# Row sums of the first head group moved from TensorE matmuls to accumulating transfers and VectorE, in a two-layer graph attention kernel

## The chip, the cores and the metric

The kernel runs on one core of a Trainium2 chip. The metric is the device time of one execution in microseconds. The version before takes 3048.53 us, the median of 3 runs (3048.48 to 3050.49).

A core has TensorE (PE, matmuls into PSUM), VectorE (DVE), ScalarE (ACT), GpSimd (POOL) and SyncE (SP). Each takes its own instructions in order and waits on semaphores for the others. Transfers are issued here from SP and from GpSimd.

## The reference

Thirty-two graphs of 512 nodes with 256 features pass two layers. `adj` is a 0/1 matrix for each graph. All arithmetic is float32.

```python
# layer 0, per graph
allowed = (adj > 0) | (adj.T > 0) | eye
q, k, v = split(x @ Wqkv.T + bqkv)                # 8 heads of 32
attn    = softmax(where(allowed, q k^T / sqrt(32), -inf))
x1      = layernorm(x + (attn v) @ Wo.T + bo) * g1 + b1
ff      = relu(x1 @ W1.T + b1) @ W2.T + b2        # hidden width 1024
x2      = layernorm(x1 + ff) * g2 + b2
x       = layernorm(x + x2)
# layer 1, per graph: attention alone, masked where adj == 0
x       = layernorm(x + attention(x, adj))
```

## The kernel before

Matrices lie with 128 rows on the 128 partitions. The eight heads form two head groups `hg` of four, so that four 32-wide heads fill the partitions. Scores are computed transposed: `scores(layer, k)` makes, for head group `k // 4` and key block `k % 4`, a 128 (keys) x 4 heads x 512 (queries) tile `s` in PSUM (L399). `exp` (ScalarE, L408) writes it to an SBUF tile `p` of 1 MB, of which there are eight buffers; `s` has one buffer, so the next scores wait for the exp. `masked` (VectorE, L412) multiplies by the 0/1 mask, and `product` (L419) accumulates values times `p` over the four key blocks into `acc`. `context` copies `acc` to `cT`.

No maximum is subtracted; the quotient is applied to `cT` at the end. The row sums run over keys, that is over the partitions and the four blocks. For each layer and head group:

- `pair` (L432), an accumulating transfer issued by GpSimd, adds one `p` tile to another; `fold` (VectorE, L435) does the same. For group 0 blocks 0 to 3 end in the tile k=2 by two pairs and a fold; for group 1 blocks 4 to 7 end in k=3's buffer by a pair and two folds.
- `sums` (L443) multiplies the folded tile by a 128x32 block of ones: four matmuls, one per head, whose result `psR` holds each head's sums repeated on 32 partitions.
- `blocks` (VectorE, L460) transposes 32x32 blocks of it into `sT`, `invert` (L463) takes the reciprocal of one column, `widen` (L471) spreads it back over 32 partitions, `divide` (L475) multiplies `cT`. `sT` has one buffer, which `blocks` and `widen` share.
- `guard` (GpSimd, L467) adds the sums and the reciprocals to a running `total`; at the end a total that isn't below a limit switches to a general version of the kernel.

In the last layer of the last graph there is no folding: `sums` runs over all four tiles.

`project` multiplies by Wo, `add`, `stats`, `aggregate`, `root` (GpSimd), `center` and `affine` are the residual and the layer norm, `hidden`, `relu` and `mlp` the feed-forward part. Dense products go through `dense` (L186) and are either one 128-wide matmul (`wide=True`) or four 32-wide ones. Their PSUM tiles share three banks with `psR`.

The order of all work is written out by hand as a list of such calls. `opening` (L551) starts the pipeline, `period` (L1366) is called 26 times with five neighbouring graphs a to e in different states, and `closing` (L1657) ends it. Nothing reorders them: each engine takes its own calls in the order of that list. A transfer is issued from the queue of the engine that its method names.

```python
folded = [2 + hg] if not self.final(layer) else range(hg * NQ, (hg + 1) * NQ)
for k in folded:
    for j in range(HPC):
        nc.tensor.matmul(ps[j * HD : (j + 1) * HD, :], ones, self.p(layer, k)[:, j, :], ...)
```

Of the kernel before, what the change touches and what calls it, by code (L numbers as in the profile page):

```python
# [27 lines left out]
def kernel(ctx: ExitStack, tc: tile.TileContext, t: dict, out: bass.AP):  # L28
# [12 lines left out]
    nc = tc.nc  # L41
# [109 lines left out]
    def plain(pools: ExitStack):  # L151
# [7 lines left out]
        def value_bias(layer):  # L159
            ps = ps_d.tile([P, D], F32, tag="d", name=f"psB_{layer}")  # L160
            bv = proj[layer][3]
            for k in range(ND):
                nc.tensor.matmul(
                    ps, bv[:, k : k + 1].to_broadcast([P, P]), wo[layer][:, k, :], start=(k == 0), stop=(k == ND - 1)
                )
            nc.vector.tensor_tensor(bov[layer], ps, bo[layer], ALU.add)

        def hidden_bias():

            ps = ps_d.tile([P, NF], F32, tag="d", name="psB_2")  # L170
            for f in range(NF):
                for c in range(ND):
                    nc.tensor.matmul(  # L173
                        ps[:, f : f + 1],
                        w1[:, c, f * P : (f + 1) * P],
                        b2_c[:, c : c + 1],
                        start=(c == 0),
                        stop=(c == ND - 1),
                    )
            nc.vector.tensor_tensor(b1, b1, ps, ALU.subtract)  # L180
            nc.vector.tensor_tensor(be1, be1, b2, ALU.add)

        def dense(out, lhsT, rhs, start, stop, wide):

            for at in (slice(0, P),) if wide else [slice(j * HD, (j + 1) * HD) for j in range(HPC)]:
                nc.tensor.matmul(out[at], lhsT[:, at], rhs, start=start, stop=stop)  # L186

# [4 lines left out]
        class Graph:  # L192
# [121 lines left out]
            def once(self, i):  # L314

                if i < 2:
                    value_bias(i)
                else:
                    hidden_bias()
# [131 lines left out]

            def sT(self, layer, hg):
                return self.at("sT", (layer, hg), [N // HD, HD], bufs=1)

# [3 lines left out]
            def blocks(self, layer, hg):  # L458

                nc.vector.transpose(self.sT(layer, hg).rearrange("p a b -> p (a b)"), self.bank("R", (layer, hg), [N]))  # L460

            def invert(self, layer, hg):
                nc.vector.reciprocal(self.r(layer, hg), self.sT(layer, hg)[:, :, 0])  # L463

            def guard(self, layer, hg, i):
                src = self.r(layer, hg) if i else self.sT(layer, hg)[:, :, 0]
                nc.gpsimd.tensor_tensor(total, total, src, ALU.add)  # L467
# [83 lines left out]
        def opening(a, b, c, d, e):  # L551

            a.load()
            a.constants(0, 4)
            a.transpose(0, 0)
            a.transpose_out(0, 0)
            a.transpose(0, 1)
            a.transpose_out(0, 1)
            a.query_key(0, 0, 0, None, wide=True)
            a.query_key(0, 1, 0, None, wide=True)  # L560
            b.flip(0)
            b.sort(0, 1, 0)
            b.sort(0, 0, 0)
            a.query_key_out(0, 0, 0, None)
            a.query_key_out(0, 1, 0, None)
            a.scores(0, 1)
            a.query_key(0, 0, 1, None)
            a.constants(22, 23)
            a.exp(0, 1)
            a.query_key_out(0, 0, 1, None)  # L570
            a.scores(0, 3)
            a.exp(0, 3)
            a.query_key(0, 1, 1, None)
            a.query_key_out(0, 1, 1, None)
            b.flip(1)
            a.scores(0, 0)
            a.exp(0, 0)
            b.sort(0, 0, 1)
            a.cast()
            a.entries()  # L580
            a.entry(1)
            a.entry(0)
            b.cast()
            a.entry(2)
            b.join(0, 0)
            a.value(0, 1)
            a.scores(0, 2)
            a.exp(0, 2)
            a.entry(3)
            a.masks(0)  # L590
            a.value_out(0, 1)
            a.masks(1)
            b.sort(0, 1, 1)
            b.sort(1, 0, 0)
            a.value(0, 0)
            b.sort(1, 1, 0)
            a.value_out(0, 0)
            a.scores(0, 4)
            a.exp(0, 4)
            a.constants(10, 12)  # L600
            b.sort(1, 0, 1)
            a.masks(2)
            b.join(1, 0)
            a.masked(0, 0)
            a.scores(0, 7)
            a.product(0, 0)
            a.masked(0, 1)
            a.masked(0, 2)
            b.sort(1, 1, 1)
            b.join(1, 1)  # L610
            a.product(0, 1)
            a.pair(0, 0)
            a.product(0, 2)
            a.masked(0, 3)
            a.pair(0, 2)
            a.exp(0, 7)
            a.scores(0, 5)
            a.product(0, 3)
            b.join(0, 1)
            a.exp(0, 5)  # L620
            b.query_key(0, 0, 1, None)
            a.context(0, 0)
            a.masked(0, 7)
            b.query_key(0, 0, 0, None)
            a.constants(4, 6)
            a.scores(0, 6)
            a.masked(0, 4)
            b.query_key_out(0, 0, 0, None)
            a.product(0, 4)
            a.masked(0, 5)  # L630
            b.value(0, 1)
            b.query_key(0, 1, 0, None)
            b.query_key_out(0, 0, 1, None)
            a.exp(0, 6)
            a.masked(0, 6)
            b.query_key_out(0, 1, 0, None)
            a.product(0, 5)
            b.query_key(0, 1, 1, None)
            a.fold(0, 2, 2, 0)
            a.sums(0, 0)  # L640
            a.fold(0, 3, 6, 7)
            a.pair(0, 4)
            b.scores(0, 2)
            b.query_key_out(0, 1, 1, None)
            b.value(0, 0)
            b.exp(0, 2)
            a.constants(6, 8)
            a.product(0, 6)
            b.value_out(0, 1)
            a.blocks(0, 0)  # L650
            a.guard(0, 0, 0)
            a.product(0, 7)
            a.constants(8, 10)
            a.invert(0, 0)
            a.widen(0, 0)
            a.fold(0, 3, 3, 4)
            a.sums(0, 1)
            a.divide(0, 0)
            a.blocks(0, 1)
            a.guard(0, 1, 0)  # L660
            b.scores(0, 1)
            a.context(0, 1)
            c.flip(1)
            a.once(0)
            b.entry(1)
            a.invert(0, 1)
            a.widen(0, 1)
            a.divide(0, 1)
            a.project(0, 0, wide=True)
            b.exp(0, 1)  # L670
            b.value_out(0, 0)
            a.bias(1)
            a.project(0, 1, wide=True)
            a.add(1, 0)
            a.stats(1, 0)
            a.once(2)
            a.add(1, 1)
            a.aggregate(1, 0)
            b.entry(2)
            a.stats(1, 1)  # L680
            a.aggregate(1, 1)
            a.add(1, 3)
            a.root(1, 0, 2)
            a.center(1, 1)
            a.add(1, 2)
            a.affine(1, 1)
            a.center(1, 0)
            b.scores(0, 0)
            a.affine(1, 0)
            a.transpose(1, 0)  # L690
            a.transpose_out(1, 0)
            a.hidden(0, 4, wide=True)
            a.stats(1, 2)
            b.exp(0, 0)
            a.relu(0, 5)
            b.entry(0)
            a.hidden(0, 6, wide=True)
            a.relu(0, 4)
            a.hidden(0, 2, wide=True)
            a.stats(1, 3)  # L700
            a.relu(0, 2)
            a.relu(0, 6)
            a.relu(0, 7)
            a.aggregate(1, 3)
            a.aggregate(1, 2)
            a.root(1, 2, 4)
            c.sort(1, 1, 0)
            a.center(1, 2)
            b.entries()
            a.relu(0, 3)  # L710
            a.affine(1, 2)
            a.hidden(0, 0, wide=True)
            a.center(1, 3)
            a.affine(1, 3)
            a.transpose(1, 1)
            b.entry(3)
            b.masks(0)
            a.relu(0, 0)
            b.masks(1)
            a.relu(0, 1)  # L720
            a.masks(3)
            b.masks(2)
            b.masked(0, 0)
            b.scores(0, 5)
            b.exp(0, 5)
            a.mlp(0)
            b.masked(0, 1)
            a.constants(12, 14)
            a.bias(0)
            b.masked(0, 2)  # L730
            b.scores(0, 3)
            b.masked(0, 5)
            a.mlp(1)
            a.add(2, 1)
            c.cast()
            a.stats(2, 1)
            a.aggregate(2, 1)
            a.transpose_out(1, 1)
            a.hidden(1, 2)
            a.relu(1, 3)  # L740
            a.relu(1, 2)
            a.add(2, 0)
            a.stats(2, 0)
            b.exp(0, 3)
            c.flip(0)
            a.hidden(1, 0)
            a.relu(1, 1)
            a.hidden(1, 4)
            d.cast()
            a.hidden(1, 6)  # L750
            a.relu(1, 6)
            c.sort(0, 1, 0)
            a.center(2, 1)
            a.aggregate(2, 0)
            c.entry(0)
            a.root(2, 0, 2)
            b.product(0, 0)
            b.product(0, 1)
            a.affine(2, 1)
            b.product(0, 2)  # L760
            a.stats(3, 1)
            a.center(2, 0)
# [2027 lines left out]
```

## Time and profile before

| | |
|---|---|
| median of 3 runs | 3048.53 us |
| the profiled execution | 3046.83 us |
| its span, first to last instruction | 3044.7 us |
| mean granted TensorE clock | 0.997 |
| busy PE, DVE, ACT, POOL | 3006.8, 2667.0, 1736.5, 947.7 us |
| one repeat of `period` (start of one output store to the next) | 93.2 us |
| psR matmuls (L443) | 1072 records, 139.7 us busy |
| accumulating transfers of `p` | 189 of 1 MB, 7.7 us to landing |

A float32 matmul leaves two records, so the 1072 records are 536 matmuls or 134 packs of four, whose four matmuls, one for each column group, run side by side. The busy time of an engine is the time in which at least one of its instructions runs; neighbours overlap a little, so the start of the next instruction comes before the end of the last.

### The profile page before, as it was taken

How to read it: one execution, taken by the hardware profiler on the slowest of the kernel's cores; microseconds unless marked ns; L12 is line 12 of the kernel's file. 1: busy time of each engine (PE TensorE's matmuls, PEld its weight loads, DVE VectorE, ACT ScalarE, POOL GpSimd, SP SyncE). 2: the span in 40 equal slices, each digit the busy share in tenths (PEclk: the TensorE clock that was granted, in tenths of full speed). 3: DMA queues.
4: the chain of work that ended last, by engine and by line, in shares of the span. 5: the costliest groups of instructions: out<-in, count | busy, mean ns of one | idle time of the engine just before them, and what ended most of it. 6: DMA issues, size and time to landing. Idle time of an engine off the chain costs nothing.

```text
span 3044.7 us, 85990 instructions
## 1 busy us (share of the span) xinstructions
PE 3006.8 (99%) x38410; PEld 1359.9 (45%) x38410; DVE 2667.0 (88%) x3524; ACT 1736.5 (57%) x2111; POOL 947.7 (31%) x1126
## 2 busy tenths in 40 slices
PE   7999999999999999999999999999999999999997
PEld 3444444444444444444444444444444444444443
DVE  4788888989888998889898898988898988988986
ACT  4555655556555555655555555556555665555554
POOL 0122333333333333333333333333333333332221
PEclk9999999999999999999999999999999999999999
DMA  7554445555455654555554455544564544554440
GB/s 164 115 111 107 104 100 109 120 112 107 94 109 110 126 110 93 102 109 124 106 108 96 108 116 120 110 97 99 109 129 103 105 100 105 119 121 100 81 91 23
DMA packets 257017, 325.32 MB, mean 107 GB/s; under 512 B 147329, under 2 KB 231425, under 8 KB 231937
## 3 DMA queue, kind: packets, MB, share of 16 engines
q0 software_dynamic: 28240, 214.97, 35.7%
q1 hardware_dynamic: 228400, 104.79, 14.8%
q8 instruction: 303, 4.96, 0.7%
q14 instruction: 74, 0.60, 0.1%
HBM read 72.23 MB, written 33.55 MB: 35 GB/s over the span
## 4 chain that ended last, share of the span: by engine, by line
PE 97%; ACT 1%; DMA 1%; DVE 0%; issue 0%; POOL 0%; SPq 0%; DVEq 0%; ACTq 0%
PE s L399 18%; PE acc L419 15%; PE psH L186 15%; PE psF L186 15%; PE psQK_None L186 11%; PE psO L186 7%; PE psV L186 7%; PE psR L443 4%; PE psQK L186 4%; PE psT L360 2%; ACT p L408 1%; DMA p<-p 0%; DMA w_L_gnn_Wqkv<-in_L_gnn_Wqkv_dram 0%; PE psB L173 0%; DVE p L435 0%
## 5 line engine op out<-in xcount | busy, mean ns | idle before, releaser
L408 ACT ACTIVATE p<-s 128x2048 f32<-128x2048 f32 x512 | 962.9, 1881 | 558.7 <-PE s L399 484.6
L412 DVE TENSOR_TENSOR p<-p,m 128x2048 f32<-128x2048 f32 x512 | 1160.5, 2274 | 40.3 <-ACT p L408 37.5
L399 PE MATMUL s<-qT,kT 32*64 32x512 f32 x8192 | 571.2, 613 | 4.9 <-ACT p L408 4.0
L419 PE MATMUL acc<-p,v 128*32 128x512 f32 x4096 | 513.7, 597 | 1.3 <-DVE p L412 1.3
L504 POOL TENSOR_SCALAR rs<-mv 128x2 f32<-128x2 f32 (+1 forms) x320 | 276.4, 864 | 700.0 <-DVE mv L499 663.3
L186 PE MATMUL psH<-xT,w_L_gnn_W 128*32 128x256 f32 (+1 forms) x8024 | 480.4, 380 | 0.7 <-ACT xT L365 0.7
L186 PE MATMUL psF<-w_L_gnn_W,hT 128*32 128x256 f32 x6704 | 466.2, 380 | 0.0
L435 DVE TENSOR_TENSOR p<-p,p 128x2048 f32<-128x2048 f32 x189 | 427.6, 2275 | 2.6 <-DMA p<-p 2.2
L467 POOL TENSOR_TENSOR total<-total,sT 128x16 f32<-128x16 f32 x128 | 191.8, 1498 | 703.6 <-DVE mv L499 399.7
L540 ACT ACTIVATE hT<-psH,c_L_gnn_b 128x256 f32<-128x256 f32 x512 | 217.5, 475 | 304.6 <-PE psH L186 293.5
L186 PEld LDWEIGHTS psH<-xT,w_L_gnn_W 128*32 128x32 f32 (+1 forms) x8024 | 262.3, 111 | 268.6 <-issue 46.2
L186 PEld LDWEIGHTS psF<-w_L_gnn_W,hT 128*32 128x32 f32 x6704 | 287.3, 116 | 197.5 <-issue 36.4
L432 POOL DMA_DIRECT2D p<-p x189 | 171.0, 905 | 653.2 <-PE acc L419 458.9
L505 POOL TENSOR_TENSOR rs<-rs,neg_half 128x2 f32<-128x2 f32 (+1 forms) x320 | 257.8, 806 | 26.7
L399 PEld LDWEIGHTS s<-qT,kT 32*64 32x64 f32 x8192 | 119.3, 130 | 310.7 <-issue 143.7
L186 PE MATMUL psQK_None<-xT,w_L_gnn_Wqkv 128*32 128x512 f32 (+1 forms) x1988 | 241.0, 595 | 4.7 <-DMA w_L_gnn_Wqkv<-in_L_gnn_Wqkv_dram 4.7
L186 PE MATMUL psO<-w_L_gnn_Wo,cT 128*32 128x256 f32 (+1 forms) x2056 | 238.5, 380 | 2.9 <-DVE cT L475 2.9
L419 PEld LDWEIGHTS acc<-p,v 128*32 128x32 f32 x4096 | 114.3, 109 | 257.8 <-issue 189.2
L186 PEld LDWEIGHTS psO<-w_L_gnn_Wo,cT 128*32 128x32 f32 (+1 forms) x2056 | 168.8, 136 | 65.7 <-issue 12.9
L496 DVE BATCH_NORM_STATS2 st<-y 128x6 f32<-128x256 f32 x384 | 158.4, 420 | 6.2
L365 ACT COPY xT<-psT 128x512 f32<-128x512 f32 x130 | 75.9, 583 | 140.1 <-PE psT L360 140.1
L493 DVE TENSOR_TENSOR y<-psO,x 128x256 f32<-128x256 f32 x256 | 102.9, 413 | 51.9 <-PE psO L186 51.4
(71 smaller groups left out, 2777.6 us busy)
## 6 DMA issues: line engine op xcount, KB each, us to landing
p<-p POOLq DMA_DIRECT2D x189, 1024.0 KB, 7.7
x<-in_x_dram SPq DMA_DIRECT2D x32, 512.0 KB, 4.2
code<-in_adj_dram POOLq DMA_DIRECT2D x32, 512.0 KB, 9.9
m<-code SPq DMA_DIRECT2D x32, 512.0 KB, 4.6
out_dram<-x SPq DMA_DIRECT2D x32, 512.0 KB, 3.8
kT<-v SPq DMA_DIRECT2D x248, 64.0 KB, 3.0
m<-code SPq DMA_TRANSPOSE x128, 4.0
w_L_gnn_W<-in_L_gnn_W_dram SPq DMA_DIRECT2D x2, 1024.0 KB, 9.4
```

Of the source, the lines that this page charges most:

```text
L186: nc.tensor.matmul(out[at], lhsT[:, at], rhs, start=start, stop=stop)
L399: nc.tensor.matmul(s[half * P // 2 : (half + 1) * P // 2, j, :], self.kT(layer)[at, hg, key : key + P // 2], self.qT(layer)[at, hg, :], st ...
L408: nc.scalar.activation(self.p(layer, k), self.at("s", (layer, k), [HPC, N]), AF.Exp, scale=SCALE)
L412: nc.vector.tensor_tensor(p, p, m[:, k % NQ, None, :].to_broadcast([P, HPC, N]), ALU.mult)
L419: nc.tensor.matmul(acc[j * HD : (j + 1) * HD, :], self.v(layer)[:, kc, h * HD : (h + 1) * HD], self.p(layer, k)[:, j, :], start=(kc == 0), ...
L432: nc.gpsimd.dma_start(out=self.p(layer, k), in_=self.p(layer, k + 1), accum_op=ALU.add)
L435: nc.vector.tensor_tensor(self.p(layer, dst), self.p(layer, a), self.p(layer, b), ALU.add)
L467: nc.gpsimd.tensor_tensor(total, total, src, ALU.add)
L496: nc.vector.bn_stats(self.at("st", (n, i), [6]), self.y(n, i))
L504: nc.gpsimd.tensor_scalar(rs, self.mv(n)[:, a:b, 1:2], EPS, None, ALU.add)
L505: nc.gpsimd.tensor_tensor(rs, rs, neg_half[:, a:b, None], ALU.pow)
L540: nc.scalar.activation(self.hT(h)[:, f, :], ps[:, f % 2, :], AF.Relu, bias=b1[:, f : f + 1])
```

## The change

Group 0 of both layers no longer uses TensorE for its sums, except in the last layer of the last graph. The folded tile is halved twice by accumulating transfers (`halve`: partitions 64 to 127 are added to 0 to 63, then 32 to 63 to 0 to 31). Four transfers (`spread`) lay head j's 32 partitions at partitions 32j of a tile `part`. `blocks` transposes `part`, and a new VectorE reduction (`reduce`) sums 32 values for each query into a small tile `total`, which `invert` and `guard` then read. Group 1 keeps its matmul. In the last layer of the last graph group 0 keeps it too, and `reduce` is a copy there.

The constants that were computed in one call (`value_bias`, `hidden_bias`) are split into a TensorE part (`once`) and a VectorE part (`once_out`). The lists `opening`, `period` and `closing` are written anew throughout: order of key blocks, of projections, of transfers, and which dense products are wide.

```diff
+        SPREAD = {(0, 0), (1, 0)}
...
+            def spread_out(self, layer, hg):
+                return (layer, hg) in SPREAD and not self.final(layer)
+
+            def halve(self, layer, hg, rows):
+                p = self.p(layer, 2 + hg)
+                nc.gpsimd.dma_start(out=p[:rows], in_=p[rows : 2 * rows], accum_op=ALU.add)
+
+            def spread(self, layer, hg, j):
+                part = self.at("part", (layer, hg), [N], bufs=1)
+                nc.sync.dma_start(out=part[j * HD : (j + 1) * HD, :], in_=self.p(layer, 2 + hg)[:HD, j, :])
+
+            def total(self, layer, hg):
+                if (layer, hg) in SPREAD:
+                    return self.at("total", (layer, hg), [N // HD], bufs=2)
+                return self.sT(layer, hg)[:, :, 0]
...
             def blocks(self, layer, hg):
-                nc.vector.transpose(self.sT(layer, hg).rearrange("p a b -> p (a b)"), self.bank("R", (layer, hg), [N]))
+                if self.spread_out(layer, hg):
+                    src = self.at("part", (layer, hg), [N], bufs=1)
+                else:
+                    src = self.bank("R", (layer, hg), [N])
+                nc.vector.transpose(self.sT(layer, hg).rearrange("p a b -> p (a b)"), src)
+
+            def reduce(self, layer, hg):
+                if self.spread_out(layer, hg):
+                    nc.vector.tensor_reduce(self.total(layer, hg), self.sT(layer, hg), AX.X, ALU.add)
+                else:
+                    nc.vector.tensor_copy(self.total(layer, hg), self.sT(layer, hg)[:, :, 0])
 
             def invert(self, layer, hg):
-                nc.vector.reciprocal(self.r(layer, hg), self.sT(layer, hg)[:, :, 0])
+                nc.vector.reciprocal(self.r(layer, hg), self.total(layer, hg))
 
             def guard(self, layer, hg, i):
-                src = self.r(layer, hg) if i else self.sT(layer, hg)[:, :, 0]
+                src = (self.total, self.r)[i](layer, hg)
                 nc.gpsimd.tensor_tensor(total, total, src, ALU.add)
```

The lists differ in nearly every line. Cut to the calls that the prediction speaks of, in their order (each "..." stands for other calls), the new opening begins, and the new period runs:

```diff
         def opening(a, b, c, d, e):
             a.load()
+            a.cast()
             a.constants(0, 4)
...
         def period(a, b, c, d, e):
+            c.halve(0, 0, P // 4)
             b.exp(1, 1)
+            a.root(4, 2, 4)
+            c.spread(0, 0, 2)
             b.masked(1, 1)
+            c.spread(0, 0, 1)
             c.fold(0, 3, 3, 4)
             b.masked(1, 3)
-            c.sums(0, 0)
             c.sums(0, 1)
             c.blocks(0, 1)
+            c.spread(0, 0, 3)
             b.scores(1, 4)
             b.exp(1, 4)
             c.invert(0, 1)
             c.widen(0, 1)
             b.masked(1, 2)
+            c.spread(0, 0, 0)
             b.scores(1, 7)
             b.product(1, 1)
             b.product(1, 2)
             c.divide(0, 1)
             c.blocks(0, 0)
+            c.reduce(0, 0)
             c.invert(0, 0)
             c.widen(0, 0)
             c.divide(0, 0)
             c.project(0, 0)
...
             b.fold(1, 2, 2, 0)
+            b.halve(1, 0, P // 2)
...
-            b.sums(1, 0)
+            b.halve(1, 0, P // 4)
+            b.spread(1, 0, 2)
...
             c.root(2, 0, 2)
             d.exp(0, 5)
+            b.spread(1, 0, 1)
+            b.spread(1, 0, 3)
             b.blocks(1, 0)
+            b.reduce(1, 0)
...
             c.transpose(2, 0)
             b.project(1, 0, wide=True)
             c.root(2, 2, 3)
             c.affine(2, 2)
             d.fold(0, 2, 2, 0)
+            d.halve(0, 0, P // 2)
             d.pair(0, 4)
```

## The prediction

> **What bounds the kernel now.** I read the page's busy shares first, then the chain that ended last, then one stage in the table of windows, then TensorE's waits, and last the timeline around the work that the change takes away.
>
> ```profile
> span 3044.7 us, 85990 instructions
> PE 3006.8 (99%) x38410; PEld 1359.9 (45%) x38410; DVE 2667.0 (88%) x3524; ACT 1736.5 (57%) x2111; POOL 947.7 (31%) x1126
> ...
> PE 97%; ACT 1%; DMA 1%; DVE 0%; issue 0%; POOL 0%; SPq 0%; DVEq 0%; ACTq 0%
> ...
> L435 DVE TENSOR_TENSOR p<-p,p 128x2048 f32<-128x2048 f32 x189 | 427.6, 2275 | 2.6 <-DMA p<-p 2.2
> ...
> p<-p POOLq DMA_DIRECT2D x189, 1024.0 KB, 7.7
> ...
> kT<-v SPq DMA_DIRECT2D x248, 64.0 KB, 3.0
> ```
>
> TensorE (PE) is busy 99% of the span and is 97% of the chain. The windows cut at two stores of the output, one repeat of the steady stage apart, say it more sharply (columns: stretch, length, then busy of PE, weight loads, VectorE, ScalarE, GpSimd, granted clock, DMA share, GB/s):
>
> ```profile
> 370.50:463.70 93.20, 93.20 (x1194) 42.23 (x1193) 83.06 (x111) 54.22 (x67) 30.90 (x36) 1.00 0.51 109
> 463.70:556.90 93.20, 93.20 (x1194) 42.22 (x1193) 83.84 (x111) 54.20 (x67) 31.29 (x36) 1.00 0.52 109
> ```
>
> PE has no gap at all in a repeat, VectorE is at 83.8/93.2 = 90%, the other engines and the DMA are far below. PE's own waits agree: they sum to about 30 us in the whole run, and the largest are single ones of the opening and the end.
>
> ```profile
> PE psT L360 <- DMA x<-in_x_dram: 5.3, 1, 5.3
> PE psQK_None L186 <- DMA w_L_gnn_Wqkv<-in_L_gnn_Wqkv_dram: 4.7, 1, 4.7
> ...
> PE psR L443 <- DVE p L435: 2.0, 1, 2.0
> ```
>
> So a microsecond of PE work removed in the steady stage is a microsecond of span, as long as no wait moves in.
>
> **A rule of the skill.** Perfetto Trace Analysis, section Identifying the Most-Contended Engine, says that the busy time of matmuls is a bad measure for how near TensorE is to its limit, because they are pipelined. It matters here in one place: what a removed matmul is worth. The group of psR records shows 139.7 us for 134 packs of four, 1.04 us a pack. But the timeline's starts say something else:
>
> ```profile
> 412.71 1.11 PE L399 MATMUL s<-qT,kT 32*64 32x512 f32 x16
> 413.76 1.06 PE L443 MATMUL psR<-p,ones 128*32 128x512 f32 x8
> 414.64 1.90 PE L186 MATMUL psQK_None<-xT,w_L_gnn_Wq 128*32 128x512 f32 x16
> ...
> 420.98 1.04 PE L443 MATMUL psR<-p,ones 128*32 128x512 f32 x8
> 421.84 1.90 PE L186 MATMUL psQK_None<-xT,w_L_gnn_Wqkv 128*32 128x512 f32 x16
> ```
>
> From the start of a psR pack to the start of what follows it is 0.88 and 0.86 us. The rest of its 1.04 us lies under the next matmul. I go by the distance of starts, not by busy time. (In front of a scores pack the distance is about 0.1 longer, but that 0.1 belongs to the scores pack: whoever then stands in front of it pays it.) For the DVE reduction, which no row shows on this shape, the second page is VectorE: DVE Perf Modes, section The perf-mode tier table: a tensor_reduce runs in the one-element-per-cycle mode only. That puts it beside this trace's one-element rows of the same 128x512 size: 712 ns (L460), 703 ns (L471), 691 ns (L475).
>
> **The change, part by part.** *Sums of the first head group.* Removed are the four psR matmuls of (layer, 0) for all 64 layer-graph pairs but the last layer of the last graph: 63 packs; the order of the changed program on PE confirms 134 psR packs before and 71 after, with every other kind of pack kept in number. Some dense products change between one 128-wide and four 32-wide matmuls. The starts price these alike (an output projection of 4 packs is 3.46/2 = 1.73 us wide, 1.73 narrow; an mlp pack 3.55 wide, 3.59 narrow ahead of scores), so I cost that at nothing. Gain on PE: 63 x 0.87 = 55 us, of it 2 x 0.87 = 1.74 us in each repeat of 93.2.
>
> *What replaces them.* Per layer: two accumulating transfers on GpSimd (64 and then 32 partitions), four plain transfers of 32 x 512 on SP (64 KB each), a transpose from SBUF instead of PSUM (703 against 712 ns, no change), and one reduction of 128x512 to 128x16. None of it is on PE.
> VectorE: +63 x about 0.65 us (between bn_stats' 0.42 on half the size and the 0.71 of a transpose) = 41 us; per repeat 83.8 + 1.3 = 85.1 of 91.4 us, 93%. Still below PE; even 1.5 us each would leave it there.
> GpSimd: +126 issues x 0.905 us (row L432) = 114 us; the guard of group 0 now reads a small packed tile and not a strided one (median 2182 ns for the strided source, 217 for r), up to 64 x 1.9 = 120 us less at best; part of that 2182 is a block behind a running VectorE tensor_tensor, so I count only half. GpSimd stays under 40%.
> DMA: the 189 accumulations and 32 casts fill 35.7% of 16 engines with 215 MB; 63 x 0.75 MB more is +8%, and the spreads +2%: about 62%. Not a bound.
>
> *The chain's lateness.* This is the only new way to stop PE, since the summed tile must be free before an exp can write its buffer and the quotients must be there before project. I laid the period out with the starts above, 0 being its begin, 91.4 its length. Layer 0: the adds before it put fold(0,2,2,0) at 78.4 to 80.6 (behind root(2,2,3) and affine(2,2)). Then halve by 64: 0.9 to issue and some 6 to land (between 3.0 for 64 KB and 7.7 for 1 MB), halve by 32: 0.9 and some 5; four spread issues x 0.6 (a sort's 64 KB issue on SP) and 3.0 to land. Sum 18.2 us, so 80.6 + 18.2 - 91.4 = 7.4 in the next repeat. Two wait for that. exp(1,4), whose buffer is the summed tile's, is due at 12.1, when its scores end; the next scores pack stands at 15.6 and needs it done (1.9), so the last moment is 13.7. And blocks(0,0), which VectorE reaches only at about 14.5. Slack 6 us. Layer 1: fold at 35 to 37, spreads landed near 54; its buffer goes to exp(0,5) at 57, and blocks(1,0) is reached at 66. Slack 3 us and more.
> The waits these bring to queues: halve by 32 stands on GpSimd waiting for halve by 64; behind it are root(4,2,4), whose readers are norm and store, and in layer 1 root(2,0,2), needed by transpose(2,0) only 20 us later. Spread waits on SP; behind it are loads, flips and sorts of later graphs, which have tens of us.
>
> *Tightest hand-off.* project(0,0) is at 18.4 on PE, right after product(1,2). VectorE before it, from masked(1,1), ready when its exp ends at 2.2: masked and fold to 6.7; masked(1,3) from 7.7 (its exp) to 10.0; blocks, invert and widen of group 1 to 11.7; masked(1,2) 13.9; divide 14.5; blocks, reduce, invert, widen and divide of group 0 to 17.3. Slack 1.1 us. I book 2 us in all for it.
>
> *The order elsewhere.* The period is written anew; the same walk finds transposes, mlp and products with 2 us of slack or more. In the opening the cast of the adjacency stands ahead of the weights: the trace has DMA at share 1.05 from 5 to 12 us while x and Wqkv come, so 1.5 MB more there delays the first projection by 1 to 4 us; masks come sooner, but PE's first products stand at 35 us in both. Two scores packs in a row (s needs the exp of 1.9 between) add 2 to 4 us; less may go in later waits, which in the old opening are 2.0, 1.9 and 3.5. The bounds are -6 and +10, I take +3. The final layer keeps its psR packs and its tail of adds, norms and store: 0.
>
> Sum: 3044.7 - 55 + 2 + 3 = 2994.7 us of span. The profiled execution took 3046.83, 2.1 around the span, so 2996.8; the median shown is 1.7 above that execution: **2998 us**.
>
> **Rivals.** (1) *The chain is late and the kernel is slower.* An accumulation into 64 or 32 partitions may land no sooner than one into 128, and each may queue behind a whole pair (7.7) and the cast (9.9). Then halve, queue, halve is 0.9 + 7.7 + 7.7 + 0.9 + 7.7 and the spreads 5.4: 30 us, ending at 19.5, 5.8 past the last moment. PE then waits at the scores pack, 5.8 - 1.7 = 4.1 us a repeat over 26: 3048 + 107 = about 3155. It decides from a landing at 15.4, 8 us later than I reckon. For it: q0 holds pairs, casts and halves together. Against it: half and a quarter of the bytes, and DMA half idle. (2) *VectorE becomes the pace at the hand-off.* At 93% it has 6 us of idle left in a repeat; if reduce takes 1.2 or the masks come 1 us late, project(0,0) waits 0.5 to 1.5 us each time: 13 to 39 us given back, 3011 to 3037. For it: the slack of 1.1. Against it: VectorE has no wait on the chain. (3) *Nothing is paid*: the opening no worse and no stall, 2988 to 2992. (4) *The sums do not leave PE*: excluded by the program's order on PE.
>
> **How the numbers follow.** My forecast with 2990 to 3008: 0.60. Rival 3 and better: 0.10. Rival 2: 0.18. Rival 1 from any lateness over the break-even: 0.09. The remaining 0.03 lies between rivals 2 and 1, within 0.2% of before (about 6 us, what a measurement of this kernel can tell). Faster 0.88, same 0.03, slower 0.09. A range of 2986 to 3030 leaves out the slow end and a little more; the forecast's own is 2990 to 3008.
>
> **What would show it.** Right: the window of one repeat is 91.3 to 91.8 us with PE busy in all of it, VectorE at about 85, 71 psR packs, a reduce of 0.5 to 0.75 us, PE's waits still near 30 us and all in the opening and the end. Wrong by rival 1: waits of scores on exp, and exp on the p<-part DMA, in every repeat. Wrong by rival 2: waits of psO on the divide. Wrong in the opening: the first projection later than 16 us, or a clock below 1.00 for longer than now.

## The result, and the profile after

| | before | after | forecast |
|---|---|---|---|
| median, us | 3047.46 (8 runs, 3045.59 to 3050.71) | 3056.93 (8 runs, 3055.61 to 3059.12) | 2998 (2986 to 3030) |
| span of the profiled execution, us | 3044.7 | 3057.1 | 2994.7 |
| PE busy, us | 3006.8 | 2976.1 | |
| one repeat of the period, us | 93.2 | 93.2 | 91.3 to 91.8 |

The ratio of after to before is 1.0031, with a 95% interval of 1.002 to 1.0042. The kernel became slightly slower, although 31 us of TensorE's busy time are gone. The forecast was wrong in sign.

From the page of the changed kernel: span and busy times, then the chain that ended last by engine, then the reduction of the folds and the transfers.

```profile
span 3057.1 us, 83051 instructions
PE 2976.1 (97%) x36442; PEld 1374.6 (45%) x36442; DVE 2706.1 (89%) x3588; ACT 1746.1 (57%) x2111; POOL 921.5 (30%) x1252
...
PE 77%; DVE 16%; issue 2%; POOL 2%; DMA 2%; ACT 1%; DVEq 0%; SPq 0%; POOLq 0%; ACTq 0%
...
L434 DVE TENSOR_TENSOR p<-p,p 128x2048 f32<-128x2048 f32 x189 | 430.9, 2281 | 9.8 <-DMA p<-p 8.5
...
p<-p POOLq DMA_DIRECT2D x189, 1024.0 KB, 7.8
p<-p POOLq DMA_DIRECT2D x63, 512.0 KB, 5.2
...
p<-p POOLq DMA_DIRECT2D x63, 256.0 KB, 5.7
part<-p SPq DMA_DIRECT2D x252, 64.0 KB, 2.1
```

TensorE is still 97% busy, but its share of the chain fell from 97% to 77%, and 16% of the chain now runs over VectorE. An engine at 89% busy has come into the chain by being late at certain moments. The halvings land in 5.2 and 5.7 us and the spreads in 2.1.

The windows, cut again at output stores, have the same columns as before (stretch, length, then busy of PE, weight loads, VectorE, ScalarE, GpSimd, granted clock, DMA share, GB/s):

```profile
463.53:556.76 93.23, 92.02 (x1118) 42.84 (x1116) 84.69 (x113) 54.55 (x67) 28.88 (x40) 1.00 0.67 131
556.76:650.00 93.24, 92.03 (x1118) 42.83 (x1116) 84.69 (x113) 54.56 (x67) 29.15 (x40) 1.00 0.69 131
```

A repeat is as long as before, but PE is busy in only 92.02 of 93.23 us. Its busy time fell by 1.18 us a repeat, and 1.21 us of idle time came in. TensorE's waits say where:

```profile
PE s L398 <- ACT p L407: 20.9, 20, 8.5
PE psH L162 <- DVE y L522: 16.5, 26, 0.6
PE psV L162 <- DVE y L522: 14.9, 26, 0.6
```

Two waits occur 26 times, once in each repeat, 0.6 us each. Neither is a wait for data: `psH` and `psV` are the *destinations* of `c.hidden(0,4)` and `c.value(1,0)`, and L522 is `add`, which reads a finished projection out of PSUM. TensorE waits until `add` has emptied the bank that it wants to write. The timeline around the first shows why `add` is late (columns: start, duration, engine, line, operation, tiles, then the idle time before and its releaser):

```profile
633.48 1.93 PE L162 MATMUL psO<-w_L_gnn_Wo,cT 128*32 128x256 f32 x32
...
636.29 2.28 DVE L411 TENSOR_TENSOR p<-p,m 128x2048 f32<-128x2048 f32 x1
...
639.92 4.49 DVE L411 TENSOR_TENSOR p<-p,m 128x2048 f32<-128x2048 f32 x2
...
642.36 1.89 PE L162 MATMUL psV<-w_L_gnn_Wqkv,xT 128*128 128x256 f32 x8
644.32 0.42 DVE L522 TENSOR_TENSOR y<-psO,x 128x256 f32<-128x256 f32 x1
...
644.88 3.48 PE L162 MATMUL psH<-xT,w_L_gnn_W 128*128 128x256 f32 x15 [0.64 <-DVE y L522]
```

The projection is finished at 635.4. Its second half, `c.add(1,3)`, stands in VectorE's queue behind three maskings of some 2.28 us and some short steps, and runs at 644.32, 9 us later. `hidden(0,4)` waits for the bank that it empties. The other wait has the same form: `b.add(4,3)` at 600.85 stands behind `d.fold(0,2,2,0)` at 597.08, and `value(1,0)` waits 0.57 us for it.

```profile
597.08 2.27 DVE L434 TENSOR_TENSOR p<-p,p 128x2048 f32<-128x2048 f32 x1
...
600.85 0.41 DVE L522 TENSOR_TENSOR y<-psO,x 128x256 f32<-128x256 f32 x1
...
601.31 1.94 PE L162 MATMUL psV<-w_L_gnn_Wv,xT 128*32 128x256 f32 x32 [0.57 <-DVE y L522]
```

The Trainium skill describes this picture (Perfetto Trace Analysis, section Optimization Strategy): the same gap, repeated, on the engine that should be saturated can mean that there isn't enough SBUF or PSUM for the next tile. The trace has the picture, 26 equal gaps at each of two places. The runs below show that order removes them with the banks as they are; no run has more banks.

Over the whole span the difference of +12.4 us divides at the first and last repeat: the opening took some 23 us longer (332.4 against 309.0), the 26 repeats under 1 us, and the closing some 11 us less (300.7 against about 312). The new period begins at another place of the pipeline, so part of this is work that only changed sides.

### The profile page after: what moved, and what is told of

Same layout as the page of the kernel before. It is cut to its first block, busy times and chain, and to the rows that moved or that the text cites. A ratio compares the mean times of both kernels' runs of the same rounds, so it can differ in the third digit from the quotient of the medians.

```text
span 3057.1 us, 83051 instructions
## 1 busy us (share of the span) xinstructions
PE 2976.1 (97%) x36442; PEld 1374.6 (45%) x36442; DVE 2706.1 (89%) x3588; ACT 1746.1 (57%) x2111; POOL 921.5 (30%) x1252
## 4 chain that ended last, share of the span: by engine, by line
PE 77%; DVE 16%; issue 2%; POOL 2%; DMA 2%; ACT 1%; DVEq 0%; SPq 0%; POOLq 0%; ACTq 0%
PE psF L162 14%; PE psH L162 14%; PE s L398 13%; PE acc L418 10%; PE psQK_None L162 9%; DVE p L411 6%; PE psV L162 6%; PE psO L162 4%; PE psQK L162 3%; DVE p L434 3%; DVE st L525 2%; PE psR L442 2%; DVE y L522 2%; PE psT L359 1%; DMA p<-p 1%
## 5 line engine op out<-in xcount | busy, mean ns | idle before, releaser
L162 PE MATMUL psH<-xT,w_L_gnn_W 128*32 128x256 f32 (+1 forms) x6200 | 472.8, 380 | 16.5 <-DVE y L522 16.5
L162 PE MATMUL psF<-w_L_gnn_W,hT 128*32 128x256 f32 (+1 forms) x6704 | 462.2, 381 | 0.0
L533 POOL TENSOR_SCALAR rs<-mv 128x2 f32<-128x2 f32 (+1 forms) x320 | 189.1, 591 | 744.6 <-DVE mv L528 728.8
L162 PEld LDWEIGHTS psH<-xT,w_L_gnn_W 128*32 128x32 f32 (+1 forms) x6200 | 300.6, 119 | 222.0 <-issue 81.4
L162 PEld LDWEIGHTS psF<-w_L_gnn_W,hT 128*32 128x32 f32 (+1 forms) x6704 | 292.2, 116 | 180.5 <-ACT hT L569 33.1
L569 ACT ACTIVATE hT<-psH,c_L_gnn_b 128x256 f32<-128x256 f32 x512 | 211.3, 473 | 220.9 <-PE psH L162 220.9
L534 POOL TENSOR_TENSOR rs<-rs,neg_half 128x2 f32<-128x2 f32 (+1 forms) x320 | 327.1, 1022 | 26.7
L431 POOL DMA_DIRECT2D p<-p x189 | 174.2, 922 | 532.5 <-PE acc L418 468.8
L458 POOL DMA_DIRECT2D p<-p x126 | 107.7, 855 | 440.3 <-DVE mv L528 196.2
L162 PEld LDWEIGHTS psO<-w_L_gnn_Wo,cT 128*32 128x32 f32 (+1 forms) x2776 | 155.3, 123 | 99.1 <-issue 45.4
L554 ACT ACTIVATE x<-z,ms,rs 128x256 f32<-128x256 f32 x128 | 73.0, 596 | 165.8 <-DVE ms L538 162.6
```

The lines of the kernel that those rows point to most:

```text
L431: nc.gpsimd.dma_start(out=self.p(layer, k), in_=self.p(layer, k + 1), accum_op=ALU.add)
L458: nc.gpsimd.dma_start(out=p[:rows], in_=p[rows : 2 * rows], accum_op=ALU.add)
L533: nc.gpsimd.tensor_scalar(rs, self.mv(n)[:, a:b, 1:2], EPS, None, ALU.add)
L534: nc.gpsimd.tensor_tensor(rs, rs, neg_half[:, a:b, None], ALU.pow)
L569: nc.scalar.activation(self.hT(h)[:, f, :], ps[:, f % 2, :], AF.Relu, bias=b1[:, f : f + 1])
```

## The experiments

The theory: the repeat is held by two releases of PSUM banks, which depend on where `add` stands in VectorE's queue. Its rivals: the removed packs never were worth 0.87 us each; the new order costs what the removal pays, and the removal could have done without it; VectorE has become the bound by its amount of work. For the opening there is a theory of its own: the transfers that replace the sums delay an exp. Each expectation names what it weighs, by letters of its own.

**One `add` moved.**

```diff
             c.add(1, 2)
+            c.add(1, 3)
...
-            c.add(1, 3)
```

> Change: in the period c.add(1, 3) follows c.add(1, 2) directly, ahead of three masked products. Theory A (two PSUM banks are freed late by VectorE adds, each wait by itself): the wait of psH on y goes (0.8 of 0.85 us a repeat), psV's stays at 0.57; repeat 92.4, time about 22 us below the changed kernel, 3035. Theory B (VectorE at 85 of 93 us is the pace, the wait only shows where): the other wait grows by as much, repeat 93.2, time within 4 us of the changed kernel, 3057.

Measured: 3184.19 us, ratio 1.0453 (1.0435 to 1.047). The `psH` wait went, and something much larger came. The timeline of this kernel, one repeat:

```profile
646.52 0.42 DVE L522 TENSOR_TENSOR y<-psO,x 128x256 f32<-128x256 f32 x1 [0.56 <-PE psO L162]
...
650.86 0.59 ACT L554 ACTIVATE x<-y,ms,rs 128x256 f32<-128x256 f32 x1
651.48 0.43 DVE L522 TENSOR_TENSOR y<-psO,x 128x256 f32<-128x256 f32 x1 [4.54 <-ACT x L554]
...
652.16 2.28 DVE L411 TENSOR_TENSOR p<-p,m 128x2048 f32<-128x2048 f32 x1
...
654.49 1.93 PE L418 MATMUL acc<-p,v 128*32 128x512 f32 x8 [3.42 <-DVE p L411]
...
656.35 2.01 PE L398 MATMUL s<-qT,kT 32*64 32x512 f32 x16
```

`add(1,3)` writes a tile `y`, and the buffer it gets is freed by `a.norm(4,0)` on ScalarE (L554), which still stood further down. So VectorE stood 4.54 us with the masking behind it, and TensorE stood 3.42 us for the masked tile. The release was one link longer than I had followed it: PSUM bank, `add`, `y` buffer, `norm`. It also cost more than its wait: by its output stores a repeat is 98.2 us on average, 5.0 more, though the 0.64 us wait of `psH` is gone. After the gap a scores pack takes 2.01 us and not 1.11, and over the repeat from 567.8 to 666.7, which is 98.9 us long, the granted clock is 0.97. The skill (TensorE: Matmul & The Clock Gate, section HAM oscillation) gives the rule that TensorE should have no idle gaps above about 3.4 us. The trace agrees in 25 of the 26 repeats, in which a stretch at half clock goes with this gap of 3.42 us. In the first repeat the same gap, ending at 362.0, is followed by a clock of 1.00 and a scores pack of 1.11 us.

**The other `add` moved, and both.**

```diff
+            b.add(4, 2)
+            b.add(4, 3)
             d.fold(0, 2, 2, 0)
```

> Change: in the period b.add(4, 2) and b.add(4, 3) stand ahead of d.fold(0, 2, 2, 0). Theory A: the wait of psV on y goes, psH's stays; repeat 92.4, about 3035. Theory B: psH's wait grows instead, repeat 93.2, about 3057. The fold and all behind it are 0.7 us later; should that be what PE waits for next, a new wait shows in the list, on exp or divide.

> Both moves. Theory A: no PE wait in the period, repeat 91.4 to 91.7, 40 to 48 us below the changed kernel, 3009 to 3017, thus 30 to 38 below the kernel before. Theory B: repeat 93 or more with other waits of PE on VectorE, 3050 or more. In between (3020 to 3045): VectorE is late at more places than these two.

Measured for the first: 3054.53 us, ratio 1.0023 (1.0014 to 1.0032). The `psV` wait is gone and `psT`, the transpose of graph c's layer-0 output, waits in its place, because `c.norm(3,2)` became late by the same reordering. The waits of that kernel:

```profile
PE psH L162 <- DVE y L522: 16.5, 26, 0.6
PE psT L359 <- ACT x L554: 15.8, 27, 0.6
```

With both moves it is 3173.55 us, ratio 1.0418 (1.0401 to 1.0436), with the large wait of the first. All three were misses in size: taking one late release away gained next to nothing, or cost much, where another instruction behind it was late as well.

**The releases moved with what stands behind them.** Next I moved `a.norm(4,0)` first, and then the adds of 4 together with what their place had made late.

```diff
             a.norm(4, 3)
+            a.norm(4, 0)
...
             c.add(1, 2)
+            c.add(1, 3)
...
-            a.norm(4, 0)
-            c.add(1, 3)
```

```diff
+            c.aggregate(3, 2)
+            b.add(4, 2)
+            b.add(4, 3)
             d.fold(0, 2, 2, 0)
...
+            c.root(3, 2, 3)
             d.halve(0, 0, P // 2)
```

The first kernel has only the first edit, the second has both.

> Change: c.add(1, 3) behind c.add(1, 2) as in the first run, and now also a.norm(4, 0), whose y buffer it takes, behind a.norm(4, 3) on ScalarE. Theory A (fixed late hand-offs in the new order, not VectorE's pace): the wait of psH goes, psV's stays; repeat 92.4, about 3035. Theory B (VectorE is the pace): a new wait of PE on VectorE of the same size, repeat 93.2, about 3057.

> The same, and c.aggregate(3, 2), b.add(4, 2), b.add(4, 3) ahead of d.fold(0, 2, 2, 0) on VectorE, c.root(3, 2, 3) ahead of d.halve(0, 0, 64) on GpSimd, so that transpose(2, 1) isn't held by norm(3, 2). Theory A: no PE wait left in the period, repeat 91.4 to 91.7, 3009 to 3017, faster than before by 1%. Theory B: repeat 92.8 or more. A third outcome, repeat about 92.4: one of the two hand-offs only moves to another reader.

Measured: 3033.19 us, ratio 0.9951 (0.9934 to 0.9968), and 3012.95 us, ratio 0.9886 (0.9869 to 0.9902), both as the theory of the releases had it. One repeat of the first and one of the second in the windows:

```profile
554.20:646.50 92.30, 91.72 (x1118) 42.83 (x1116) 84.43 (x113) 54.49 (x67) 28.78 (x40) 1.00 0.69 132
```

```profile
553.10:644.70 91.60, 91.60 (x1118) 42.94 (x1116) 84.52 (x113) 54.49 (x68) 32.20 (x40) 1.00 0.70 133
```

Averaged over 22 stores the repeats are 92.36 and 91.58 us. So the `psH` wait was worth 0.87 us a repeat and the `psV` wait 0.78, though the records show 0.64 and 0.57. TensorE's packs in the first of the two kernels, at the place where the changed kernel has its `psH` gap, show where the difference lies:

```profile
639.76 1.89 PE L162 MATMUL psV<-w_L_gnn_Wqkv,xT 128*128 128x256 f32 x8
641.49 5.34 PE L162 MATMUL psH<-xT,w_L_gnn_W 128*128 128x256 f32 x24
```

`psH` starts 1.73 us after the start of `psV` here, 0.16 us before the end of it. In the changed kernel it starts 2.52 us after it, so a recorded gap of 0.64 delays it by 0.79. The rest of the 0.87 is the `psH` packs, which take 5.27 us to the next start here and 5.35 there.

With both waits gone PE has no gap left in the repeat, and its length is what the forecast gave for it. The chain of the second kernel says the same:

```profile
PE 94%; DMA 2%; DVE 1%; ACT 1%; issue 1%; POOL 1%; SPq 0%; DVEq 0%; POOLq 0%; ACTq 0%
```

**The sums put back into the new order.** In the 26 repeats group 0 is summed by matmuls again, while everything else stays as changed. The halvings and spreads are left out there, and the reduction becomes a copy.

```diff
-                return (layer, hg) in SPREAD and not self.final(layer)
+                steady = 3 <= self.b <= 28 if layer == 0 else 2 <= self.b <= 27
+                return (layer, hg) in SPREAD and not self.final(layer) and not steady
...
+            c.sums(0, 0)
             c.blocks(0, 0)
...
+            b.sums(1, 0)
             b.blocks(1, 0)
```

> The new order, but in the 26 repeats the sums of group 0 are matmuls again (52 packs back on TensorE, no halving, no spreading, the reduction a copy of one column). Theory A: the two packs stand ahead of the two waits and fill them; repeat 93.2 to 93.7, time 3055 to 3070, so the removal is worth almost nothing in this order. If the removal still saves its 1.74 us a repeat beside the waits: repeat 95.0, time about 3102. Theory B expects below 93.2, as VectorE is relieved of 0.4 us and of waits on transfers.

Measured: 3108.39 us, ratio 1.0202 (1.0185 to 1.0219). The waits stayed, `psH` 17.0 and `psV` 15.0 us over 26, so my expectation that the packs would fill them was a miss. A repeat is 95.18 us by its stores: the removal pays 95.18 - 93.23 = 1.95 us a repeat, 51 us in all, somewhat more than its price of 1.74. The new order with the same work costs 95.18 - 93.22 = 1.96 us a repeat against the old one. The two waits are 1.65 of that; no run isolates the other 0.3. Removal and new order together, without the two waits, take off 93.22 - 91.58 = 1.64 us.

**The removal in the old order.** The other corner of the square: the lists of the kernel before, in the 26 repeats with halving, spreading and reducing, group 0's steps moved behind those of group 1.

```diff
+            c.halve(0, 0, P // 2)
...
+            c.halve(0, 0, P // 4)
...
-            c.sums(0, 0)
-            c.blocks(0, 0)
...
-            c.invert(0, 0)
-            c.widen(0, 0)
-            c.divide(0, 0)
...
+            c.spread(0, 0, 0)
+            c.spread(0, 0, 1)
+            c.spread(0, 0, 2)
+            c.spread(0, 0, 3)
+            c.blocks(0, 0)
+            c.reduce(0, 0)
+            c.invert(0, 0)
+            c.widen(0, 0)
+            c.divide(0, 0)
```

Layer 1 is edited in the same way.

> The old lists, opening and closing as before; in the 26 repeats the sums of group 0 by halve, spread and reduce (52 packs off TensorE), with blocks to divide of group 0 moved behind those of group 1. Theory A (the removal pays wherever it is put; the new order is what cost): repeat 91.5 to 92.0, 3001 to 3015. Rival C (the chain of 18 us doesn't fit the old order): PE waits for divide or for exp on a buffer of the chain, repeat above 93.2, time above 3047.

Measured: 3112.31 us, ratio 1.0209 (1.0192 to 1.0226). Its waits:

```profile
PE psO L186 <- DVE cT L505: 57.1, 28, 3.1
PE psQK L186 <- DVE y L523: 29.3, 26, 1.5
```

The projection waits some 2 us a repeat for the quotients, and `psQK` 1.1 us for a bank that an `add` has to empty: a late release once more. The transfers explain little of it directly, since VectorE waits for the spreads only 15 times, 12.3 us in all. In the repeat from 469.3 to 564.4 the projection waits for group 0's five steps on VectorE, which end at 528.2 and stand behind those of group 1. So in this arrangement the old order doesn't hide the removal. That no arrangement of it would is not shown: one was tried.

**The opening.** The one large single wait of the changed kernel is 8.51 us at 193.05, a scores pack whose exp needs the buffer of a tile still being added up by `a.pair(1,4)`. On GpSimd's queue that transfer stands behind the second halving, which waits for the first. The timeline of GpSimd and of ScalarE:

```profile
173.76 0.91 POOL L458 DMA_DIRECT2D p<-p  x1 [8.93 <-DVE p L434]
...
180.85 0.89 POOL L458 DMA_DIRECT2D p<-p  x1 [1.92 <-DMA p<-p]
181.57 1.10 POOL L431 DMA_DIRECT2D p<-p  x1
...
191.12 1.88 ACT L407 ACTIVATE p<-s 128x2048 f32<-128x2048 f32 x1 [11.35 <-DMA p<-p]
```

First, graph 0's layer 1 alone is summed by matmuls again:

```diff
-                return (layer, hg) in SPREAD and not self.final(layer)
+                return (layer, hg) in SPREAD and not self.final(layer) and not (self.b == 0 and layer == 1)
...
+            a.sums(1, 0)
```

> The changed kernel, but graph 0 in layer 1 (its chain lies in the opening) sums group 0 by a matmul. Theory D (the opening's single wait of 8.5 us is a pair that stands on GpSimd behind a halve that waits for the halve before it): the wait at 193 us goes or falls below 2 us, and the clock dip with it; 7 to 11 us below the changed kernel, 3046 to 3050. Rival (the pair is late for other reasons): wait of 6 us or more stays, 3055 or more.

Measured: 3053.3 us, ratio 1.002 (1.0013 to 1.0028), 3.6 us below the changed kernel. The wait fell to 4.49 us and did not vanish: the pair was now issued at 177.83, and its own way to landing keeps the exp. That theory was half right: the halvings cost 4 us of the wait, and the rest stayed with the pair alone. Then the kernel with both releases repaired, with that pair ahead of the second halving and the sums still off TensorE:

```diff
+            a.pair(1, 4)
             a.halve(1, 0, P // 4)
...
-            a.pair(1, 4)
```

> The kernel of e6 with one move in the opening: a.pair(1,4) ahead of the second halving a.halve(1,0,P//4), so that GpSimd issues the pair transfer before it stands and waits for the first halving. Theory A (the opening's stall is order on GpSimd's queue): e8 took 3.6 us off by taking the halvings away altogether; with the pair ahead of one of them some 2 to 3.5 us go, so 3009.5 to 3011 us against 3013 for e6, the repeat unchanged at 91.57. Theory B (the halving that is now later makes the chain late for the sums of graph 0, layer 1): the wait comes back at another place, 3013 us or above.

Measured: 3008.97 us (3005.23 to 3010.98), ratio 0.9876 (0.9859 to 0.9892), 4.0 us below the kernel without this move, a little more than the 2 to 3.5 expected. The wait is 3.93 us and was 8.9, and the repeat is still 91.6. This is the best version of the study, 1.2% faster than the kernel before and 1.6% faster than the changed one.

**The reduction twice.** The changed kernel with its one new VectorE instruction doubled.

```diff
                     nc.vector.tensor_reduce(self.total(layer, hg), self.sT(layer, hg), AX.X, ALU.add)
+                    nc.vector.tensor_reduce(self.total(layer, hg), self.sT(layer, hg), AX.X, ALU.add)
```

> The changed kernel with its 128x512 reduction done twice, which adds 63 instructions of 0.686 us, 43.2 us of VectorE in all, 1.37 us a repeat. Theory A (the two waits are set by an instruction's place in VectorE's queue, and VectorE has gaps of its own behind both reductions, 1.0 us at 632 us and 1.3 us at 684 us of the profiled execution, where it waits for TensorE): the gaps take it up, 0 to 0.3 us a repeat, 3057 to 3064 us. Theory B (VectorE, 90% busy in the period, has become the bound, so that the work added for the sums is itself what ate the gain): 1.1 to 1.4 us a repeat, 3085 to 3093 us.

Measured: 3059.12 us, ratio 1.0047 (1.003 to 1.0064), which overlaps the changed kernel's 1.002 to 1.0042. The profiled span is 3057.3 against 3057.1 us. One repeat:

```profile
554.70:647.90 93.20, 92.00 (x1118) 42.87 (x1116) 86.02 (x115) 54.53 (x67) 29.33 (x40) 1.00 0.70 131
```

VectorE has 1.33 us more to do in each repeat (86.02 against 84.69), and the repeat is no longer. VectorE's amount of work is out as the bound: what holds TensorE is the place of two instructions in VectorE's queue and not the amount of work in it.

## Why the prediction was wrong

The forecast's sum and what the profiled executions show, in us of span:

| step | forecast | measured |
|---|---|---|
| the period: waits that came in | +2 | +42.9 |
| opening: waits and clock | +3 | +14.2 |
| closing: waits and clock | 0 | +5.0 |
| work removed from TensorE, what is left of the sum | -55 | -49.7 |
| sum | -50 | +12.4 |

The period's line is the 1.65 us a repeat that the two repairs gave back, 26 times. In the first 300 us TensorE's waits sum to 29.8 us against 21.6, and it was busy for 22.0 us at half clock against 10.0, of which half is lost. In the last 300 us the waits are 11.6 us against 8.4, with 3.4 us at half clock against none. The last line can be checked apart: the repaired repeats are 1.64 us shorter than before, 42.6 us in all, and the 11 packs outside them come to 9.6 us at 0.87, together 52.

- *Sums of the first head group*: right. 71 packs are left, and putting the packs back cost 1.95 us a repeat against 1.74 forecast. The distance of starts was the right price: with the sums put back, the two packs hold 0.86 and 0.97 us, and the pack ahead of the second gives back 0.11, 1.72 in all. Of the other 0.23, 0.19 is the output projection, which starts 1.93 us after the products ahead of it and not 1.74; its cause isn't traced.
- *What replaces them*: right in what it bounds. The reduction takes 0.686 us (0.65 forecast), close to VectorE's transposes of that size (0.70 to 0.72). VectorE is at 84.7 us a repeat (85.1), and DMA's share at 0.67 to 0.69 (0.62). GpSimd became less busy, 921.5 against 947.7 us, where the forecast came to some 54 us more. Its doubt about the guards was well placed and too small, as the last section shows.
- *The chain's lateness*, rival 1: right to reject it in the period. The halvings land in 5.2 and 5.7 us and the spreads in 2.1, where 6, 5 and 3.0 were reckoned, and no scores pack waits for an exp there. In the opening the same mechanism was real, though: that is the 8.51 us wait, which I had walked through for the period alone.
- *Tightest hand-off*, rival 2: `project(0,0)` doesn't wait in the period at all. The doubled reduction shows that VectorE has room there.
- *The order elsewhere*: this is the step that failed. "The same walk finds transposes, mlp and products with 2 us of slack or more" followed each product's inputs. It did not follow its destination: which of the three banks it gets, which `add` has to empty that bank, and what stands ahead of that `add` on VectorE. With the sources ready, the two products still started late, 26 times each. The walk was also silent on `hidden` and `value`, the two kinds that wait. So it put at nothing what cost 1.65 us a repeat, 43 of the 50 us that were forecast as the gain.
- The opening: +3 was the wrong size, with bounds of -6 to +10 that were too narrow. Of the +14.2, 8.2 are waits and 6.0 the clock. The one wait of 8.51 us, by GpSimd's order and then the pair's landing, is as large as the whole increase of waits, and the half clock around its end costs 2.6 us. Why TensorE is busy at half clock for 16.8 us before 100 us, and for 10.0 before the change, stays open. The closing's 5.0 is seen only in the trace: the largest piece is a scores pack that waits 2.62 us at 2802 for an exp held by a transfer, with 1.7 us by the clock behind it.
- The 0.09 given to "slower" was all on rival 1. The loss came by a mechanism that had no case of its own.

Repaired at the two releases, the kernel has the repeat of 91.6 us that the forecast named; with the opening's pair moved it comes to 3009 us, and about 11 us above the forecast remain in the opening and the closing.

## What to carry to other kernels

When an order is written anew and buffers rotate, walk each matmul's destination as carefully as its inputs: find who must release that bank, what stands ahead of the releaser in its own queue, and which buffer the releaser itself needs. Before you move a late releaser, look for its second link: of two such moves alone one cost 127 us and the other gained next to nothing, until the instructions behind the next release were moved too. On the pages, the saturated engine's share of the chain fell from 97% to 77% while its busy share only fell from 99% to 97%. Here that was the sign of small, regular releases that come late.

## What the runs showed of the hardware

- A wait of TensorE costs more than its record. Waits of 0.64 and 0.57 us were worth 0.87 and 0.78 us a repeat when they were taken away. For the first, the trace shows most of the difference: without the wait the next pack starts 0.16 us before the end of the one ahead, and that overlap is lost as well.
- The same gap doesn't always lower the clock. In the first experiment the gap of 3.42 us that ends at 362.0 is followed by 10 us at a granted clock of 1.00; behind the one that ends at 458.0 the clock over 10 us is 0.83, and behind the one that ends at 654.5 it is 0.52 over 6.5 us. Gaps of 2.62 us in two closings differ too: in the changed kernel (at 2802) the next scores pack takes 1.56 us, and in the kernel with both releases repaired (at 2760) 1.12 us. What decides isn't shown.
- An accumulating transfer within SBUF lands in 7.8 us with 1024 KB and in 5.2 with 512 KB. The 256 KB ones have two lengths behind their median of 5.7: 4.9 us for the one issued at 560.41, while no 1 MB transfer is under way, and 7.2 for the one issued at 605.17, behind a pair issued at 601.47. The partitions halve with the bytes, from 64 to 32; no run separates the two.
- A small GpSimd instruction can last as long as a large one of VectorE beside it. In the kernel before, 80 of the 128 guards that read `sT` start within or at most 0.1 us ahead of a 128x2048 `tensor_tensor` of VectorE. All 80 take over 1 us and end within 0.1 us of the end of such an instruction; the 48 others take 0.2 to 0.4 us. So it was this, and not the strided source, that made their median 2182 ns.
